# Dilated attention and a binary depthwise convolution on one core: group statistics of the packed blocks sent through DRAM, zero edges written by ScalarE, and a new table of places

## The chip, the cores and the metric

The kernel runs on one core of a Trainium2 chip. The metric is the device time of one launch in microseconds (us), taken as the median of several runs. For the kernel before the change it is 5095.06 us (three runs, 5094.93 to 5096.68). One more execution was taken with the hardware profiler; every row quoted below comes from it.

## The reference, cut to what matters

The input x has 16 images of 56 x 56 pixels and 384 channels, float32. Two layers follow each other, each with a residual:

```python
x = x + attention(_gn(x), w_qkv, w_proj, b_proj)   # layer 0
x = x + depthwise3x3(_gn(x), sign(clip(w)))        # layer 1

def _gn(v, G=32, eps=1e-5):        # no affine part; one mean and variance per image and group of 12 channels
    g = v.reshape(B, H, W, G, C // G)
    return ((g - mean(g, (1, 2, 4))) / sqrt(var(g, (1, 2, 4)) + eps)).reshape(v.shape)
```

The attention has three channel groups of 128 with dilations 1, 2 and 3. In each, four heads of 32 channels look at nine neighbours: score = sum over a head's channels of q times the shifted k, softmax over the nine, then the weighted sum of the shifted v, then a 384 x 384 projection. The convolution multiplies each channel with nine taps that are -1, 0 or 1. Outside the picture k, v and the normalised input of the convolution are zero.

## The kernel before, in words

**Chunks.** An image is cut into 7 chunks of 8 rows (448 pixels); channels lie on the partitions, in three blocks of 128. So there are 112 chunks, and each goes through three stages, written as generators:

- *A* (`plan_a`): load x (L471), transpose it on TensorE (`pt_x`, L476), copy it out (ScalarE, L489), take its statistics (VectorE, L491), store it channel-major in DRAM as `xd` (L494).
- *B* (`plan_b`): load (L520), normalise (ScalarE, L524); project k and v (`pkv`, L528, copied out by ScalarE, L541) and exchange halo rows with the chunk before by small DMAs (L549, L550); project q (`pq`); nine score products on VectorE (`t`, L593), each 128 x 1344; sum them over channels on TensorE (`ps`, L574, in bursts of 8, 8 and 11 matmuls); softmax (L613 to L648, with a transposing DMA L646); spread the weights over channels (`pb_a`, L660), multiply with v on VectorE (`w`, L671), add on GpSimd (L681 to L685); project (`po`, L699), add residual and bias (L703), take the statistics of the result (L707), store it as `x1d` (L710).
- *C* (`plan_c`), ten chunks behind B: channel blocks 0 and 1 are convolved partly on TensorE. They are loaded from `x1d` as "packed" blocks `z` of 96 partitions (L770): 32 channels in three vertically shifted copies, four sets of 32 channels beside each other. ScalarE applies scale and offset to z (L786), TensorE multiplies with diagonal matrices (`pc`, L818), VectorE adds the middle column of taps (L829 to L835). Block 2 goes over ScalarE (L860, L882) and GpSimd (L892 to L900). The result is transposed back (`pt_o`, L909), copied (L915) and stored (L918).

**Statistics.** `group_norm` turns 12-channel statistics into scale and offset per channel. It runs once per image (for layer 1 of image b and layer 0 of image b+2 together) and crosses the engines: L352 VectorE, `pm` TensorE (L358), L360 VectorE, `pb` TensorE (L365), L368 VectorE, L370 and L371 GpSimd, `pv` TensorE (L376), L380 to L384 VectorE, thirteen tiny GpSimd operations for the inverse root (L387 to L391, tile `pair`), `pp` TensorE (L396), and `mr` (L399, VectorE), which has scale and offset for each of 128 channels. The packed z needs the same numbers on 96 partitions, three times: that is `mrz`. Before the change 24 tiny matmuls compute it a second time (`pz`, L408) and VectorE copies it out of PSUM (L414).

**Zero edges.** In the first and last chunk of an image one row of z lies outside the picture. GpSimd writes zeros there after the load (L775) and again after the normalisation (L789), since the offset makes them nonzero.

**Order.** Engines execute their queues in order. The order is written out by hand: `WHEN` gives each step of each stage a place; a chunk takes nine places (STEP = 9), so a step of chunk m stands at 9m plus its place (C: 9(m + 10) plus its place). `put` registers the steps, and from place 0 to place 9 x 112 + 14 each engine is held to that order (`pin`). Only the order counts; the places are no waits. A list of several numbers belongs to one generator, which is advanced one `yield` at each. The places of `statistics` are counted from the last chunk of the image.

**Buffers.** PSUM tiles with the tag "mt" (`pkv`, `po`, `pt_x`, `pt_o`, `pc`, `pt_s` and all the statistics') share three banks; `pq`, `pb_a` and `ps` have one each. SP issues nearly all DMAs, in order, over eight semaphores in turn.

Of the kernel before, what the change touches and what calls it, by code (L numbers as in the profile page):

```python
# [8 lines left out]
F32 = mybir.dt.float32  # L9
# [8 lines left out]
P = 128  # L18
HEADS = 4
HD = 32  # L20
NG = 3
NTAP = 9
NQ = 4
# [8 lines left out]
TERMS = 3  # L32

WHEN = dict(
    load_in=[[1.86]],
    turn_in=[[6.026, 7.853, 8.103, 9.616], [8.887, 8.898, 11.431, 13.527], [9.427, 9.669, 9.841, 12.978]],
    load_x=[[-16.698]],
    normalise=[[-14.8], [-11.887], [-14.8]],
    k=[[-7.795, -7.784, -7.773], [-6.349, -6.338, -2.8], [-3.845, -3.158, -1.177]],
    v=[[7.341, 7.352, 8.827], [5.08, 6.207, 9.429], [7.847, 8.378, 9.967]],  # L40
    query=[[4.619], [7.271], [8.939]],
    score=[[4.825], [5.138], [5.149], [7.626], [7.637], [7.877], [10.723], [10.734], [10.745]],
    burst=[[5.75], [8.056], [11.108]],
    softmax=[[11.283, 12.017, 12.028, 12.151, 13.101, 13.445, 14.191, 14.202, 14.629, 15.664]],
    weigh=[[17.248, 17.838, 20.379], [18.267, 18.278, 20.39], [20.023, 20.034, 20.421], [20.194, 20.223,
        23.104], [20.709, 20.932, 24.835], [21.886, 22.889, 25.743], [23.429, 23.44, 25.754], [23.902, 25.371,
        27.079], [25.884, 25.895, 27.807]],
    load_residual=[[28.002]],
    out_project=[[28.362, 28.749, 29.829, 108.842], [28.647, 29.405, 34.465, 55.401], [30.355, 30.533, 31.612,
        34.476]],  # L50
    load_g=[[9.822]],
    normalise_g=[[10.839]],
    taps=[[11.121, 12.433], [11.132, 12.731], [11.143, 14.144]],
    sums=[[18.53], [18.541], [18.813]],
    load_x1=[[5.837]],
    load_z=[[-1.661, 3.083], [1.74, 3.075]],
    normalise_z=[[5.379, 5.39], [7.123, 7.821]],
    column=[[6.427], [7.222]],
    convolve=[[5.632, 6.438], [8.054, 8.065]],
    turn_out=[[19.405, 19.416, 19.866], [20.439, 20.499, 20.51], [21.786, 21.835, 27.008], [22.192, 22.518,  # L60
        22.582]],
    statistics=[[33.116, 34.74, 35.945, 35.956, 37.004, 37.015, 37.026, 37.993, 38.004, 39.539, 40.578, 40.589,
        40.926, 40.937, 41.368]],
)
C_SHIFT = 0
FIXED_ENGINES = ("PE", "DVE", "Activation", "Pool", "SP")
# [3 lines left out]
def dilated_attention_then_binary_conv(  # L70
# [28 lines left out]
    nc = tc.nc  # L99
    B, H, W, C = x.shape  # L100
    PX = ROWS * W
    NCH = H // ROWS
# [4 lines left out]
    K3 = 3 * HD  # L107
    JG = NG - 1
# [10 lines left out]
    ps_mt = ctx.enter_context(tc.tile_pool(name="ps_mt", bufs=3, space=PSUM))  # L119
# [5 lines left out]
    ident = const.tile([P, P], F32, name="ident")  # L125
# [13 lines left out]
    for p in range(NPAD):  # L139

        v = place(p) if p < NG * NTAP else p
# [202 lines left out]
    def group_norm(sets):  # L344

        L = len(sets)
        ch = st_p.tile([P, L, NG, 2], F32, tag=f"ch{L}", name="ch")
        for only_first in (False, True):
            for n, (stats, _, for_convolution) in enumerate(sets):
                if for_convolution == only_first:  # L350
                    for j in range(NG):
                        nc.vector.bn_aggr(ch[:, n, j, :], stats()[:, j].rearrange("p c s -> p (c s)"))  # L352
            yield

        pair = st_p.tile([GN_G, L, 3], F32, tag=f"pair{L}", name="pair")
        pm = ps_mt.tile([P, 512], F32, tag="mt", name="pm")
        for j in range(NG):
            nc.tensor.matmul(pm[:GN_G, 0:L], gsel[:, j], ch[:, :, j, 0], start=(j == 0), stop=(j == NG - 1))  # L358
        yield
        nc.vector.tensor_scalar_mul(pair[:, :, 2], pm[:GN_G, 0:L], -1.0 / GN_CH)  # L360
        yield

        pb = ps_mt.tile([P, 512], F32, tag="mt", name="pb")
        for j in range(NG):
            nc.tensor.matmul(pb[:, j * L : (j + 1) * L], gselT[:, j], pair[:, :, 2], start=True, stop=True)  # L365
        yield
        dev = st_p.tile([P, L, NG], F32, tag=f"dev{L}", name="dev")
        nc.vector.tensor_tensor(dev, pb[:, : NG * L].rearrange("p (j l) -> p l j", l=L), ch[:, :, :, 0], ALU.add)  # L368
        yield
        nc.gpsimd.tensor_tensor(dev, dev, dev, ALU.mult)  # L370
        nc.gpsimd.tensor_tensor(dev, dev, ch[:, :, :, 1], ALU.add)  # L371
        yield

        pv = ps_mt.tile([P, 512], F32, tag="mt", name="pv")
        for j in range(NG):
            nc.tensor.matmul(pv[:GN_G, 0:L], gsel[:, j], dev[:, :, j], start=(j == 0), stop=(j == NG - 1))  # L376
        yield
        var = st_p.tile([GN_G, 3, L], F32, tag=f"var{L}", name="var")
        v, r, t = var[:, 0], var[:, 1], var[:, 2]
        nc.vector.tensor_scalar(v, pv[:GN_G, 0:L], 1.0 / GN_CH, 1e-5, op0=ALU.mult, op1=ALU.add)  # L380

        ri = r.bitcast(I32)
        nc.vector.tensor_single_scalar(ri, v.bitcast(I32), 1, op=ALU.arith_shift_right)
        nc.vector.tensor_scalar(ri, ri, -1, RSQRT_BITS, op0=ALU.mult, op1=ALU.add)  # L384
        yield
        for step in range(3):
            nc.gpsimd.tensor_tensor(t, r, r, ALU.mult)  # L387
            nc.gpsimd.tensor_tensor(t, t, v, ALU.mult)
            nc.gpsimd.tensor_scalar(t, t, -0.5, 1.5, op0=ALU.mult, op1=ALU.add)
            nc.gpsimd.tensor_tensor(pair[:, :, 1] if step == 2 else r, r, t, ALU.mult)  # L390
        nc.gpsimd.tensor_tensor(pair[:, :, 0], pair[:, :, 2], pair[:, :, 1], ALU.mult)  # L391
        yield

        pp = ps_mt.tile([P, 512], F32, tag="mt", name="pp")
        for j in range(NG):
            nc.tensor.matmul(pp[:, 2 * L * j : 2 * L * (j + 1)], gselT[:, j], pair[:, :, 0:2], start=True, stop=True)  # L396
        yield
        mr = st_p.tile([P, NG, L, 2], F32, tag=f"mr{L}", name="mr", bufs=5 - L)
        nc.vector.tensor_copy(mr.rearrange("p j l s -> p (j l s)"), pp[:, : 2 * L * NG])  # L399
        yield  # L400
        mrz = None
        if sets[0][2]:

            pz = ps_mt.tile([P, 512], F32, tag="mt", name="pz")
            for s in range(JG * NQ):
                of_set = gselT[:, s // NQ, s % NQ * HD : s % NQ * HD + HD]
                for ky in range(3):
                    nc.tensor.matmul(  # L408
                        pz[ky * HD : (ky + 1) * HD, 2 * s : 2 * s + 2], of_set, pair[:, 0, 0:2], start=True, stop=True
                    )  # L410
        yield
        if sets[0][2]:
            mrz = st_p.tile([K3, JG, NQ, 2], F32, tag="mrz", name="mrz")
            nc.vector.tensor_copy(mrz.rearrange("p j q s -> p (j q s)"), pz[:K3, : 2 * JG * NQ])  # L414
        yield
        for n, (_, done, for_convolution) in enumerate(sets):
            done(mr[:, :, n], mrz) if for_convolution else done(mr[:, :, n])
# [92 lines left out]
    def plan_b(m, t0):  # L510
# [180 lines left out]
        def out_project(j):  # L691

            if c == 0 and j == 0:
                stats1[b] = st_p.tile([P, NG, NCH, 6], F32, tag="stats1", name="stats1")
                x1d[b] = dr_p.tile([C, H * W], F32, tag="x1d", name="x1d")
            xr = had["xr"]
            po = ps_mt.tile([P, 512], F32, tag="mt", name="po")
            for g in range(NG):
                nc.tensor.matmul(  # L699
                    po[:, :PX], wprojT[:, g, j * P : (j + 1) * P], had[f"y{g}"], start=(g == 0), stop=(g == NG - 1)  # L700
                )
            yield
            nc.vector.scalar_tensor_tensor(  # L703
                xr[:, j, :], po[:, :PX], bias[:, j : j + 1], xr[:, j, :], op0=ALU.add, op1=ALU.add
            )
            yield
            nc.vector.bn_stats(stats1[b][:, j, c, :], xr[:, j, :])  # L707
            yield
            if j == NG - 1:
                nc.sync.dma_start(chunk_of(x1d[b], c), xr)  # L710
# [24 lines left out]
    def plan_c(m, t0):  # L735
# [2 lines left out]
        p0 = c * PX  # L738
        had = {}

        def edges(j):
            found = []
            for z, _, _ in had[f"z{j}"]:
                if c == 0:
                    found.append(z[0:HD, :, 0:W])
                if c == NCH - 1:
                    found.append(z[2 * HD : 3 * HD, :, PX - W : PX])
            return found

        def set_of(j, q):  # L750
            return next(z[:, q - q0] for z, q0, q1 in had[f"z{j}"] if q0 <= q < q1)
# [1 line left out]
        def load(j):  # L753
# [17 lines left out]
                        z[ky * HD : (ky + 1) * HD, :, lo:hi], by_set[:, q0:q1, n0 + lo : n0 + hi]  # L771
                    )
            yield
            for edge in edges(j):
                nc.gpsimd.memset(edge, 0.0)  # L775

        def normalise(j):
            mrz = mr1[b][1]
# [6 lines left out]
                    continue  # L785
                nc.scalar.activation(z, z, AF.Identity, bias=mrz[:, j, q, 0:1], scale=mrz[:, j, q, 1:2])  # L786
            yield
            for edge in edges(j):
                nc.gpsimd.memset(edge, 0.0)  # L789

        lo, hi = (0 if c else 1), ROWS + (2 if c < NCH - 1 else 1)

# [248 lines left out]
```

## Time and profile before

| what | value |
|---|---|
| median of three runs | 5095.06 us |
| profiled execution | 5091.71 us, of it the span of the core 5089.7 us |
| busy share: PE, DVE, ACT, POOL | 96%, 87%, 49%, 84% |
| a chunk without statistics, in the middle | 42.20 us |
| the two chunks with statistics, in the middle | 43.50 and 46.70 us |
| seven chunks of an image, in the middle | 301.2 us or 302.9 us, about in turn |
| first softmax copy (L613), last one | at 110.7 us, at 4877.9 us |

The chunk times are distances between the copies of L613, of which there is one per chunk. PE, DVE, ACT, POOL and SP are TensorE, VectorE, ScalarE, GpSimd and SyncE; PEld is TensorE's weight load. A group row of the page has line, engine, operation, out<-in with shapes and count, then busy time in us and the mean of one in ns, then the idle time of the engine just before such instructions and what ended it. A float32 matmul leaves two records. In the stretches view each row is one stretch: its length, then busy time and count of instructions by engine, the granted clock of TensorE (1.00 is full), and the DMA share.

### The profile page before, as it was taken

The page shows a single profiled execution, that of the slowest core. Times are in us where ns is not written, and L with a number is a line of the kernel's source. Part 1 is how long each engine was busy: PE and PEld are TensorE (multiplying, and loading weights), DVE is VectorE, ACT ScalarE, POOL GpSimd, SP SyncE. Part 2 cuts the span into 40 slices and gives each one's busy share as a digit, 9 for nine tenths or more (in the row PEclk, how much of TensorE's full clock was granted, in tenths as well). Part 3 has the DMA queues.
Part 4 walks back from the last instruction along what each step waited for, and adds up shares of the span by engine and source line. Part 5 has one row for each costly group of instructions (what it writes and reads, how often), then busy time and mean ns, then how long its engine had stood idle before and what let it go on. Part 6 is the DMA issues. An engine that isn't in the chain of part 4 may idle for free.

```text
span 5089.7 us, 72426 instructions
## 1 busy us (share of the span) xinstructions
PE 4883.7 (96%) x25093; PEld 2242.3 (44%) x25093; DVE 4434.3 (87%) x4575; ACT 2476.1 (49%) x4365; POOL 4253.3 (84%) x2998
## 2 busy tenths in 40 slices
PE   6899999999999999999999999999999999999975
PEld 4344444444444444444444444444444444444422
DVE  3788998989989998998989899898998999888866
ACT  3122555545555455555555555454555545455445
POOL 2566888888888988988888898888888888899981
PEclk8999999999999999999999999999999999999976
DMA  5334666666666666666666566666666666555555
GB/s 161 110 111 117 171 174 173 175 174 177 175 173 170 166 176 173 177 174 172 175 167 179 160 182 173 171 176 172 176 175 173 172 167 175 152 151 148 137 131 165
DMA packets 813955, 836.43 MB, mean 164 GB/s; under 512 B 362643, under 2 KB 782870, under 8 KB 813590
## 3 DMA queue, kind: packets, MB, share of 16 engines
q1 hardware_dynamic: 805606, 819.81, 60.1%
q10 hardware_dynamic: 7984, 12.00, 0.7%
q8 instruction: 199, 3.26, 0.3%
q14 instruction: 166, 1.36, 0.1%
HBM read 477.43 MB, written 231.21 MB: 139 GB/s over the span
## 4 chain that ended last, share of the span: by engine, by line
PE 78%; DVE 6%; POOL 5%; issue 2%; ACT 2%; DMA 2%; SPq 0%; ACTq 0%; DVEq 0%; POOLq 0%
PE pkv L528 24%; PE po L699 13%; PE pq L528 13%; PE ps L574 10%; PE pc L818 6%; PE pb_a L660 5%; PE pt_o L909 3%; PE pt_x L476 3%; DVE w L671 3%; POOL w L681 2%; DVE t L593 2%; PE pt_s L617 1%; ACT z L786 1%; POOL m L892 1%; DMA z<-x1d 1%
## 5 line engine op out<-in xcount | busy, mean ns | idle before, releaser
L681 POOL TENSOR_TENSOR w<-w 128x1344 f32<-128x1344 f32 x672 | 2052.2, 3054 | 448.4 <-DVE w L671 438.4
L671 DVE TENSOR_TENSOR w<-pb_a,v 128x1344 f32<-128x1344 f32 x1008 | 1562.7, 1550 | 347.0 <-PE pb_a L660 302.5
L593 DVE TENSOR_TENSOR t<-pq,k 128x1344 f32<-128x1344 f32 x1008 | 1512.8, 1545 | 56.5 <-PE pq L528 46.3
L528 PE MATMUL pkv<-xn,wqkvT 128*128 128x448 f32 x3924 | 1553.8, 541 | 0.0
L528 PEld LDWEIGHTS pkv<-xn,wqkvT 128*128 128x128 f32 x3924 | 727.8, 190 | 648.0 <-issue 617.6
L699 PE MATMUL po<-y,wprojT 128*128 128x448 f32 x2016 | 824.6, 546 | 18.6 <-POOL y L685 18.0
L528 PE MATMUL pq<-xn,wqkvT 128*128 128x448 f32 x1962 | 811.4, 550 | 0.0
L574 PE MATMUL ps<-t,sel 128*32 128x448 f32 x6048 | 664.7, 549 | 36.6 <-DVE t L593 36.4
L892 POOL TENSOR_TENSOR m<-m 128x1344 f32<-128x1344 f32 x210 | 639.0, 3043 | 10.8 <-ACT m L882 1.5
L786 ACT ACTIVATE z<-z,mrz 96x448 f32<-96x448 f32 x840 | 570.2, 751 | 101.8 <-DVE mrz L414 97.1
L882 ACT ACTIVATE m<-zg,ktap 128x448 f32<-128x448 f32 x945 | 540.4, 655 | 9.8 <-ACT zg L860 0.4
L541 ACT COPY v<-pkv 128x448 f32<-128x448 f32 x336 | 179.0, 533 | 742.2 <-DVE w L671 380.7
L699 PEld LDWEIGHTS po<-y,wprojT 128*128 128x128 f32 x2016 | 369.2, 192 | 320.0 <-issue 283.2
L528 PEld LDWEIGHTS pq<-xn,wqkvT 128*128 128x128 f32 x1962 | 350.3, 192 | 253.8 <-issue 253.5
L541 ACT COPY k<-pkv 128x448 f32<-128x448 f32 x336 | 180.1, 536 | 547.2 <-PE pkv L528 547.2
L685 POOL TENSOR_TENSOR y<-y,w 128x448 f32<-128x448 f32 x336 | 381.8, 1136 | 26.3
L684 POOL TENSOR_TENSOR y<-w 128x448 f32<-128x448 f32 x336 | 381.3, 1135 | 26.2
L660 PE MATMUL pb_a<-aT,spread 24*128 24x448 bf16 x3024 | 369.5, 360 | 20.6 <-DVE w L671 18.6
L660 PEld LDWEIGHTS <-spread 24*128 24x128 bf16 x3024 | 100.3, 91 | 636.8 <-issue 627.5
L489 ACT COPY xa<-pt_x 128x448 f32<-128x448 f32 x315 | 167.8, 534 | 433.7 <-PE pt_x L476 406.0
L818 PE MATMUL pc<-z,kdiag 96*32 96x440 f32 x3360 | 358.0, 544 | 16.5 <-POOL z L789 15.5
L574 PEld LDWEIGHTS ps<-t,sel 128*32 128x32 f32 x6048 | 190.4, 110 | 390.6 <-issue 293.4
(141 smaller groups left out, 4649.7 us busy)
## 6 DMA issues: line engine op xcount, KB each, us to landing
z<-x1d SPq DMA_DIRECT2D x570, 224.0 KB, 5.2
xr<-xd SPq DMA_DIRECT2D x112, 672.0 KB, 4.5
x1d<-xr SPq DMA_DIRECT2D x112, 672.0 KB, 5.4
xn<-xd SPq DMA_DIRECT2D x109, 672.0 KB, 4.9
xin<-in_x_dram SPq DMA_DIRECT2D x105, 672.0 KB, 8.2
xd<-xa SPq DMA_DIRECT2D x315, 224.0 KB, 2.6
out_dram<-osb SPq DMA_DIRECT2D x420, 168.0 KB, 2.4
x<-x1d SPq DMA_DIRECT2D x80, 560.0 KB, 4.2
```

Of the source, the lines that this page charges most:

```text
L528: nc.tensor.matmul(dst[:, :PX], wqkvT[:, cc, o0 : o0 + P], had["xn"][:, cc, :], start=(cc == 0), stop=(cc == NG - 1))
L574: return nc.tensor.matmul(had["ps"][32 * j : 32 * j + 32, :PX], sel[:, s0 : s0 + 32], tk, start=(issued[j] == 1), stop=(issued[j] == len(r ...
L593: nc.vector.tensor_tensor(t.rearrange("p k (r w) -> p k r w", w=W), q3, k3, ALU.mult)
L660: return nc.tensor.matmul(pb[:, kx, :PX].rearrange("p (s n) -> p s n", s=NSUB), spread[rows_of, v % 2, :], had["a"][rows_of, :, v // 8, :] ...
L671: nc.vector.tensor_tensor(w.rearrange("p k (r w) -> p k r w", w=W), pb[:, :, :PX].rearrange("p k (r w) -> p k r w", w=W), three(kv[1][g][m ...
L681: nc.gpsimd.tensor_tensor(w0, w0, w, ALU.add)
L685: nc.gpsimd.tensor_tensor(y, y, w0[:, 2], ALU.add)
L699: nc.tensor.matmul(po[:, :PX], wprojT[:, g, j * P : (j + 1) * P], had[f"y{g}"], start=(g == 0), stop=(g == NG - 1))
L786: nc.scalar.activation(z, z, AF.Identity, bias=mrz[:, j, q, 0:1], scale=mrz[:, j, q, 1:2])
L818: return nc.tensor.matmul(pcr[q * HD : (q + 1) * HD, :, x0:x1], kdiag[:, kx // 2, j * NQ + q, :], rows(set_of(j, q))[:, :, x0 + kx - 1 : x ...
L882: nc.scalar.activation(rows(t[:, kx]), zp[:, ky : ky + ROWS, kx : kx + W], AF.Copy, scale=ktap[:, JG, o : o + 1])
L892: nc.gpsimd.tensor_tensor(had["m"], had["m"], t, ALU.add)
```

## The change

- `mrz` is no longer computed by `pz`. SP writes the first two channel blocks of `mr` to a DRAM tile `mrd` (128 x 2 x 2 numbers), and in the next step reads it back into `mrz` with three DMAs, one for each vertical shift.
- `zero` replaces `edges`: ScalarE copies a block of zeros out of the identity matrix into the edge, at the same two steps. Nothing of the packed blocks is left on GpSimd.
- `out_project` looks up the residual tile one step later, so that the projection may stand ahead of the residual's load.
- All places are new. The numbers in the diff are of the steps that the text speaks of.

```diff
-    k=[[-7.795, -7.784, -7.773], [-6.349, -6.338, -2.8], [-3.845, -3.158, -1.177]],
+    k=[[-1.772, -1.287, -0.448], [0.602, 0.693, 0.86], [1.389, 1.4, 3.364]],
-    query=[[4.619], [7.271], [8.939]],
-    score=[[4.825], [5.138], [5.149], [7.626], [7.637], [7.877], [10.723], [10.734], [10.745]],
+    query=[[8.972], [10.387], [12.844]],
+    score=[[9.067], [9.078], [9.773], [10.398], [11.394], [12.106], [13.128], [13.334], [13.447]],
...
-    load_x1=[[5.837]],
-    load_z=[[-1.661, 3.083], [1.74, 3.075]],
-    normalise_z=[[5.379, 5.39], [7.123, 7.821]],
-    column=[[6.427], [7.222]],
-    convolve=[[5.632, 6.438], [8.054, 8.065]],
+    load_x1=[[12.088]],
+    load_z=[[4.532, 8.639], [18.154, 18.373]],
+    normalise_z=[[11.361, 11.372], [19.211, 19.222]],
+    column=[[12.191], [16.571]],
+    convolve=[[12.055, 12.746], [20.473, 20.484]],
...
-    statistics=[[33.116, 34.74, 35.945, 35.956, 37.004, 37.015, 37.026, 37.993, 38.004, 39.539, 40.578, 40.589,
-        40.926, 40.937, 41.368]],
+    statistics=[[38.5, 42.48, 42.607, 43.359, 44.23, 44.622, 44.633, 44.887, 45.025, 45.117, 45.558, 45.569,
+        45.58, 46.991, 47.002]],
...
         mrz = None
         if sets[0][2]:
-
-            pz = ps_mt.tile([P, 512], F32, tag="mt", name="pz")
-            for s in range(JG * NQ):
-                of_set = gselT[:, s // NQ, s % NQ * HD : s % NQ * HD + HD]
-                for ky in range(3):
-                    nc.tensor.matmul(
-                        pz[ky * HD : (ky + 1) * HD, 2 * s : 2 * s + 2], of_set, pair[:, 0, 0:2], start=True, stop=True
-                    )
+            mrd = dr_p.tile([P, JG, 2], F32, tag="mrd", name="mrd")
+            nc.sync.dma_start(mrd, mr[:, :JG, 0, :])
         yield
         if sets[0][2]:
             mrz = st_p.tile([K3, JG, NQ, 2], F32, tag="mrz", name="mrz")
-            nc.vector.tensor_copy(mrz.rearrange("p j q s -> p (j q s)"), pz[:K3, : 2 * JG * NQ])
+            for ky in range(3):
+                nc.sync.dma_start(
+                    mrz[ky * HD : (ky + 1) * HD], mrd.rearrange("(q c) j s -> c j q s", c=HD)
+                )
...
-            xr = had["xr"]
             po = ps_mt.tile([P, 512], F32, tag="mt", name="po")
...
             yield
+            xr = had["xr"]
             nc.vector.scalar_tensor_tensor(
...
-        def edges(j):
-            found = []
+        def zero(j):
             for z, _, _ in had[f"z{j}"]:
                 if c == 0:
-                    found.append(z[0:HD, :, 0:W])
-                if c == NCH - 1:
-                    found.append(z[2 * HD : 3 * HD, :, PX - W : PX])
-            return found
+                    edge, lo = z[0:HD, :, 0:W], 0
+                elif c == NCH - 1:
+                    edge, lo = z[2 * HD : 3 * HD, :, PX - W : PX], 2 * HD
+                else:
+                    continue
+                at_ = 0 if lo else 2 * HD
+                none = ident[lo : lo + HD, at_ : at_ + W].unsqueeze(1)
+                nc.scalar.copy(edge, none.to_broadcast([HD, edge.shape[1], W]))
...
-            for edge in edges(j):
-                nc.gpsimd.memset(edge, 0.0)
+            zero(j)
```

TensorE's order of one chunk in the middle, before and after (x3 and so on are matmuls; the chunk begins with the softmax's transposes):

```
before: pt_s4 po3 pt_o3 pb_a3 pt_o3 pq3 pkv6 pb_a3 pc8 ps8 pb_a3 pt_x4 pq3 pkv6 pb_a3 pc8 ps8 pb_a3 pt_x4 pq3 pb_a3
        pt_x4 pkv3 po3 pt_o3 po3 pb_a3 ps11 pb_a3 pt_o3 pkv3 pb_a3
after:  pt_s4 pkv3 pq3 pb_a3 pt_o3 pt_o3 po3 pkv3 pt_o3 pt_x4 pb_a3 pt_x4 pt_o3 pq3 pkv3 pb_a3 ps8 pc8 pb_a3 pkv6 pb_a3
        pc8 ps8 pb_a3 pq3 po6 pb_a3 ps11 pb_a3 pkv3 pb_a3 pt_x4
```

The statistics' groups on TensorE stand before: pm ahead of a pb_a, pb one group later, pv after the last po, and in the next chunk pp after the second pt_o, then pq3, pz24. After: pm ahead of the last pkv; in the next chunk pt_s4, pb, pkv3, pv, pq3 pb_a3 pt_o3 pt_o3 po3, pp, pkv3.

## The prediction on record

> **What bounds the kernel now.** I read the busy shares and slices first, then stretches of single chunks, then TensorE's timeline where a chunk is longer, then the waits.
>
> ```profile
> PE 4883.7 (96%) x25093; PEld 2242.3 (44%) x25093; DVE 4434.3 (87%) x4575; ACT 2476.1 (49%) x4365; POOL 4253.3 (84%) x2998
> ...
> PE   6899999999999999999999999999999999999975
> ...
> PEclk8999999999999999999999999999999999999976
> ```
>
> PE is busy at 90% or more from the third slice to the 38th; only there can time be won in bulk. Busy is not yet full, so next come three stretches in the middle: a plain chunk and the two with statistics.
>
> ```profile
> 1618.70:1660.90 42.20, 42.20 (x215) 19.25 (x214) 38.84 (x38) 22.30 (x40) 37.20 (x22) 1.00 0.68 179
> 1660.90:1704.40 43.50, 42.69 (x229) 19.88 (x227) 39.97 (x49) 22.42 (x41) 37.81 (x37) 1.00 0.64 172
> 1704.40:1751.10 46.70, 45.11 (x271) 21.23 (x272) 39.38 (x41) 23.01 (x43) 42.10 (x32) 1.00 0.60 161
> ```
>
> In a plain chunk PE has no gap: 42.20 of 42.20 us, and its groups follow each other at fixed distances (three accumulated float32 matmuls every 2.26 us). So a plain chunk is worth what TensorE issues. The two chunks with statistics take 1.3 and 4.5 us more, 5.8 per image. TensorE's timeline shows where the second part is lost:
>
> ```profile
> 1705.27 0.83 PE L396 MATMUL pp<-pair,gselT 32*128 32x4 f32 x6 [1.57 <-POOL pair L391]
> 1706.03 2.52 PE L528 MATMUL pq<-xn,wqkvT 128*128 128x448 f32 x6
> 1708.48 0.68 PE L408 MATMUL pz<-pair,gselT 32*32 32x2 f32 x48
> ...
> 1714.88 1.68 PE L818 MATMUL pc<-z,kdiag 96*32 96x440 f32 x16 [0.72 <-POOL z L789]
> ```
>
> pp stands idle for the end of GpSimd's inverse root, and pc for GpSimd's zero edge. The waits of the whole run say that this is so for every image:
>
> ```profile
> ACT z L786 <- DVE mrz L414: 97.1, 15, 7.6
> ...
> POOL z L789 <- ACT z L786: 41.2, 15, 8.4
> ...
> PE pp L396 <- POOL pair L391: 30.9, 17, 4.0
> ```
>
> (total us, times, longest). In nearly every second image something follows that no wait shows:
>
> ```profile
> 2006.48:2007.90 1.42, 1.42 (x8) 1.22 (x9) 1.00 (x3) 1.03 (x3) 1.42 (x1) 1.00 0.08 22
> 2007.90:2011.30 3.40, 3.40 (x5) 1.02 (x4) 0.15 (x1) 0.00 (x0) 3.32 (x2) 0.50 0.83 229
> ```
>
> The granted clock falls to 0.50 for 3.4 us right behind the late pp. That image takes 302.9 us instead of 301.2.
>
> **What the Trainium skill says.** "TensorE: Matmul & The Clock Gate", section "What's actually happening": the clock is halved after a window of about 3.4 us with little activity and restored after a busy one; the windows run freely. The trace agrees (0.50 for 3.4 us), and free windows explain why only some images are hit. "DMA: Bandwidth & Descriptors", section "Anatomy of one DMA": about 2.0 us are fixed, most of it the receipt of the last write. The shortest median from issue to landing here is 1.8 us (k halo, 29 KB). The same page, section "Two DMAs through the same engine are not ordered": a dependent DMA must be issued behind a wait for the first one's semaphore, so SP itself will wait for `mrd`; no row of before shows such a pair.
>
> **The change part by part.** One set of statistics per image, 16 in all, 15 of them beside dense PE work.
>
> *pz leaves TensorE.* From pq's start to pz 2.45 us and from pz to pkv 0.605; without pz, pq to pkv is 2.27. Gain 0.79 x 15 = 11.8 us. L414's 0.16 us on VectorE is covered by PE.
>
> *pp's wait.* 1.84 us from the transpose ahead of it, 0.11 where nothing is missing: 1.73 x 15 = 26.0 us, if the new places cover it. Now pv to pp are pq, pb_a, two pt_o and a po: 0.3 + 2.37 + 0.30 + 0.70 + 2.35 = 6.0 us. Between them must fit: pv's result (0.4), VectorE's three small operations (0.55), GpSimd's root, which in the trace runs from 1701.85 to 1705.21 (3.35 us), and what GpSimd has ahead of the root: one of L897 and L900, 2.3 us behind L371. L371 ends some 0.6 us ahead of pv's turn, so the root begins at +1.6 us and pp may start at +5.0: covered, 1 us to spare. pv itself has only a pkv (2.26 us) behind pb in which VectorE (L368) and GpSimd (0.5 us) must answer: they do by about 1.7. What is late next is the w that GpSimd adds between root and softmax rest; aT is issued at about 15 us from the chunk's start instead of 11, lands after 4.0 us (its median), and pb_a needs it at 23.
>
> *The half clock.* Seven such windows begin at a pp (499, 1404, 2008, 2612, 3216, 3820 and 4718 us). At 1.67 us each: 11.7 us. They go with the wait.
>
> *pc's wait.* 1.08 us against 0.29 after a pb_a: 0.79 x 15 = 11.8 us. What takes its place is `mrz` through DRAM. From the chunk's start (pt_s): pp at 9.7, mr at 10.8, so SP issues `mrd` at 11. In SP's order out, two halo DMAs, aT, xd, x1d and two halo DMAs stand between it and `mrz`; aT waits for GpSimd until 15, and at 1.5 us for aT and about 0.5 for each other, the three `mrz` go at 18.9 to 19.9. SP's wait for `mrd` is covered by aT. Landing: 256 runs of 8 bytes each. The nearest rows are 384 single numbers in 5.1 us (small, 1.5 KB) and the fixed 2.0 us; I take 4.3 between them. So `mrz` is there at 24.2. ScalarE then does four z (0.65 apart), one xn and the edge, and pc can start at 28.1. The edge has no row: a copy of 448 takes 0.534 us and one of 384 0.469, so 224 take about 0.31, and I bound it by 0.28 (GpSimd's memset) and 0.53. PE reaches this pc at 25.9 plus 2.1 of statistics = 28.0. With 2.0 for the landing pc waits for nothing, with 5.1 for 0.9. I charge 0.5 x 15 = 7.5 us. Queued behind z on ScalarE are two copies of v, u and the nine tap products; their readers on PE come 5 us later.
>
> *Edges off GpSimd.* 136 memsets, 0.28 us each: 34 us of GpSimd time, but PE sets the pace, so nothing beyond pc's wait. ScalarE is at 49%; it gains the same count at 0.31. In the tail GpSimd's four waits for z_last (22.7 us) go, too.
>
> *New places in plain chunks.* The same groups stand on PE. Summed with the distances of before: twelve projections at 2.26, nine pb_a at 0.30, ps 1.5 + 1.5 + 2.27, two pc at 1.5, pt_x 3 x 0.44, pt_o 1.4, pt_s 0.49, and 0.1 for each of eight changes from float32 to pb_a: 42.2 us, as before. Gain nothing, if nothing is late. I followed the tightest cover: the second pq stands at 12.6 us from pt_s and needs the third t of the first group. VectorE starts mx at 0.64, then sub, bn, w, sum, reciprocal (5.28), t, mul, t, residual, w, and the third t from 10.8 to 12.4. Slack 0.2 us. I charge 0.05 x 100 chunks = 5 us.
>
> *Start and end.* Chunks ahead of the first C chunk are about 40.2 us now although PE has 37.3 us of work; their waits are for t, and the new order shortens them by my ledger by about 0.5: gain 4 us. In the tail two DMA hops stand between mr and z_last (about +7), and against it the column scalars are computed ahead of GpSimd's tap sums and the waits for zero edges are gone (-7). I take 0 with 12 either way.
>
> Sum: -11.8 - 26.0 - 11.7 - 11.8 + 7.5 + 5 - 4 = -52.8; half of the residual doubts of fifteen sets (0.3 us more each for a late link of the chain) gives back 5: -48. Against the profiled execution, 5091.7 - 48 = 5043.7; the median lies 3.35 us above that execution, so 5047.
>
> **The rivals.**
>
> *The hop is slow.* If `mrz` needs 8 us to land (the 1152 numbers of 4.5 KB took 10.6), pc waits 3.8 us, and the gap halves the clock in every second image (1.67): 15 x (3.8 - 0.5) + 7 x 1.67 = 61 us back: 5108 at that end, 5083 at 6 us of landing. For it: `mrd` and `mrz` are of 8-byte runs, and DMA engines are 64% busy. Against: few bytes, and 5.1 us was measured at the kernel's start beside large loads. I take 5083 for this case.
>
> *The plain chunk stalls (slower).* The place is the second pq behind the third t. If VectorE's run from mx to that t ends over 0.2 us later than I count, PE waits in each of about 105 chunks; from 0.66 us (a stall of 0.46) the 48 us are gone, and at 0.9 the time is 5047 + 0.7 x 105 = 5120. For it: VectorE is busy 38.84 of 42.20 us and has five kinds of work in this run, with ScalarE's exponential and copies between. Against: each of its distances is measured, and the order of before, as tightly laid, has no gap at all.
>
> *Better than that.* No residual wait, and start and end gain what the waits there show: 5030.
>
> *The change does not do what it says* can't be for pz and the edges: they are gone from the orders.
>
> **How the numbers follow.** Forecast 5047: 0.60, own range 5032 to 5064. Better, 5030: 0.10. Slow hop, 5083: 0.15, about half of it within the band. Stalling chunk, 5120: 0.15. A measurement of this kernel can tell about 0.2% (10 us) from no change. So faster 0.60 + 0.10 + 0.08 = 0.78, same 0.07, slower 0.15. The range leaves out most of the slower case and the end of the better one: 5024 to 5098.
>
> **What would show it.** Plain chunks of 42.2 us; an image of about 298.5 instead of 301.2 or 302.9; no L408 group; pp no longer waiting for pair; no 0.50 window behind pp; pc waiting under 1 us for z; `mrz` landing in 3 to 5 us. I am wrong if pq or ps wait for t in every chunk, if z waits for DMA mrz far beyond 24 us from pt_s, or if the tail behind the last softmax copy (212 us now) grows by over 15.

## The result and the profile after

The changed kernel takes 5064.3 us, the median of six runs (5061.2 to 5066.8). Beside runs of the kernel before on the same chip (median 5096.4, six runs) the ratio is 0.994, with a 95% interval of 0.992 to 0.995. It is faster by about 32 us; 48 had been forecast. The profiled execution took 5065.0 us (span 5063.3), against 5091.7 for that of before: these 26.7 us are what the parts below are held against. One of the five runs with ScalarE's edges alone, at 9224 us and a granted clock of 0.817, was in a slow state; the ratio of that kernel is of the other four.

The busy lines of the page, as shown of before (engines with us, share and count; then tenths in 40 slices):

```profile
PE 4883.1 (96%) x24325; PEld 2249.2 (44%) x24325; DVE 4455.8 (88%) x4559; ACT 2524.2 (50%) x4501; POOL 4224.4 (83%) x2862
...
PE   7899999999999999999999999999999999999965
...
PEclk9999999999999999999999999999999999999976
```

TensorE is as long busy as before, in a shorter span. The 768 small matmuls of pz, 11.4 us of busy time before, are gone, but the others together are busy that much longer. The three stretches, from pt_s to pt_s (a chunk with the first of the statistics, the chunk with all the rest, a plain chunk; span and PE's busy time first):

```profile
1929.38:1971.98 42.60, 42.60 (x221) 19.70 (x220) 40.10 (x46) 23.83 (x43) 37.49 (x21) 1.00 0.64 176
1971.98:2018.30 46.32, 44.98 (x234) 20.96 (x233) 39.65 (x43) 24.24 (x45) 40.02 (x39) 1.00 0.69 162
2018.30:2060.60 42.30, 42.30 (x215) 19.45 (x214) 39.16 (x40) 22.82 (x41) 37.92 (x24) 1.00 0.67 179
```

Statistics now cost 0.3 us over a plain chunk in one chunk and 2.4 to 4.0 in the next, instead of 1.7 and 4.2 to 5.9. The plain chunk has no gap but is 0.1 us longer than before. TensorE's timeline in the middle chunk (start, us, then in brackets the idle time and who ended it):

```profile
1981.82 0.83 PE L397 MATMUL pp<-pair,gselT 32*128 32x4 f32 x6
1982.57 2.52 PE L526 MATMUL pkv<-xn,wqkvT 128*128 128x448 f32 x6
...
1994.61 1.69 PE L817 MATMUL pc<-z,kdiag 96*32 96x440 f32 x16 [1.19 <-ACT z L749]
...
2001.75 1.68 PE L817 MATMUL pc<-z,kdiag 96*32 96x440 f32 x16 [0.15 <-ACT z L749]
```

pp follows its po at the ordinary distance of 0.47 us, in all fifteen images of the middle, and no window of clock 0.50 begins between 200 and 4790 us. The second pc, whose blocks need `mrz`, is 0.15 us late. The first, which still belongs to the previous image and doesn't need this `mrz`, is 1.19 us late; over fifteen images this first wait is anything from nothing to 1.4.

Where the time went, from the starts of the score transpose pt_s in both traces (us):

| stretch | before | after | difference |
|---|---|---|---|
| start to the first pt_s | 112.9 | 104.4 | -8.5 |
| nine chunks without convolution | 378.9 | 371.8 | -7.2 |
| the other 102 chunks | 4387.3 | 4356.3 | -31.0 |
| last pt_s to the end | 210.5 | 230.8 | +20.3 |
| span | 5089.7 | 5063.3 | -26.4 |

Two thirds of what the middle gains are given back at the end.

### The profile page after: what moved, and what is told of

It is laid out like the page before. It is cut to its first block, busy times and chain, and to the rows that moved or that the text cites. A ratio compares the mean times of both kernels' runs of the same rounds, so it can differ in the third digit from the quotient of the medians.

```text
span 5063.3 us, 70210 instructions
## 1 busy us (share of the span) xinstructions
PE 4883.1 (96%) x24325; PEld 2249.2 (44%) x24325; DVE 4455.8 (88%) x4559; ACT 2524.2 (50%) x4501; POOL 4224.4 (83%) x2862
## 4 chain that ended last, share of the span: by engine, by line
PE 86%; DVE 4%; DMA 4%; POOL 2%; ACT 2%; SPq 2%; issue 1%; ACTq 0%; DVEq 0%; POOLq 0%
PE pkv L526 27%; PE pq L526 15%; PE po L696 14%; PE ps L572 11%; PE pc L817 6%; PE pb_a L658 5%; PE pt_x L474 3%; PE pt_o L908 3%; DVE t L591 2%; DMA xd<-xa 1%; DVE w L669 1%; PE pt_s L615 1%; ACT z L786 1%; POOL w L679 1%; DMA mrz<-mrd 0%
## 5 line engine op out<-in xcount | busy, mean ns | idle before, releaser
L591 DVE TENSOR_TENSOR t<-pq,k 128x1344 f32<-128x1344 f32 x1008 | 1542.2, 1549 | 100.6 <-PE pq L526 98.8
L526 PE MATMUL pkv<-xn,wqkvT 128*128 128x448 f32 x3924 | 1593.0, 547 | 0.0
L696 PE MATMUL po<-y,wprojT 128*128 128x448 f32 x2016 | 808.3, 546 | 8.8 <-POOL y L683 8.8
L891 POOL TENSOR_TENSOR m<-m 128x1344 f32<-128x1344 f32 x210 | 639.6, 3046 | 27.3 <-ACT m L881 19.1
L611 ACT COPY sT<-ps 128x448 f32<-128x448 f32 x112 | 59.8, 534 | 894.8 <-PE ps L572 894.8
L526 PEld LDWEIGHTS pq<-xn,wqkvT 128*128 128x128 f32 x1962 | 354.4, 190 | 312.7 <-issue 300.4
L658 PE MATMUL pb_a<-aT,spread 24*128 24x448 bf16 x3024 | 368.9, 359 | 23.9 <-DVE w L669 22.6
L914 ACT COPY osb<-pt_o 112x384 f32<-112x384 f32 x420 | 199.1, 474 | 291.9 <-PE pt_o L908 284.3
L636 POOL TENSOR_TENSOR rest<-ew,e 112x512 f32<-112x512 f32 x112 | 129.9, 1159 | 240.1 <-ACT e L633 240.1
```

The lines of the kernel that those rows point to most:

```text
L526: nc.tensor.matmul(dst[:, :PX], wqkvT[:, cc, o0 : o0 + P], had["xn"][:, cc, :], start=(cc == 0), stop=(cc == NG - 1))
L591: nc.vector.tensor_tensor(t.rearrange("p k (r w) -> p k r w", w=W), q3, k3, ALU.mult)
L658: return nc.tensor.matmul(pb[:, kx, :PX].rearrange("p (s n) -> p s n", s=NSUB), spread[rows_of, v % 2, :], had["a"][rows_of, :, v // 8, :] ...
L696: nc.tensor.matmul(po[:, :PX], wprojT[:, g, j * P : (j + 1) * P], had[f"y{g}"], start=(g == 0), stop=(g == NG - 1))
L891: nc.gpsimd.tensor_tensor(had["m"], had["m"], t, ALU.add)
```

## The experiments

Times are medians; ratios, with their 95% intervals, are to the kernel before on the same chip (5092 to 5094 us there). The theory at the outset: the new places take the waits away, the hop through DRAM is paid at the end, ScalarE's edges hardly matter.

### The three parts, each undone or done alone

**New places alone**: the table of places of after in the kernel before, with the later lookup of the residual tile; pz on TensorE and edges by GpSimd.

```
-WHEN = dict(load_in=[[1.86]], ...
+WHEN = dict(load_in=[[16.753]], ...
```

> The kernel before with the new places alone: pz stays on TensorE, the zero edges on GpSimd. Theory A (the places give the gain of the middle; the DRAM hop makes the end longer): the start gains about 16 us as in the changed kernel, the waits of pp and pc and the half clock go, pz still costs 0.79 us an image, the plain chunk is 42.30 us, and the stretch behind the last softmax copy stays near 212 us: in all 5053 to 5060. Theory B (the longer end comes with the new places, whose last image is planned 5.6 steps later): that stretch is about 230 us here too, and the time about 5075.

Measured: 5131.6 us, ratio 1.007 (1.006 to 1.009). Slower than before, against both theories. The start gained its 17 us, pp waits no more, but the 102 chunks took 4431 us instead of 4387. GpSimd's waits show why (line waited for: us in all, times, longest):

```profile
POOL z L790 <- ACT z L787: 228.9, 60, 10.2
```

In front of its memset of the zero edge GpSimd stands and waits for ScalarE's scaled block, 60 times, 3.8 us in the mean. In the kernel before the same memset had 41.2 us, 15 times.

**The changed kernel with pz again**:

```
-            mrd = dr_p.tile([P, JG, 2], F32, tag="mrd", name="mrd")
-            nc.sync.dma_start(mrd, mr[:, :JG, 0, :])
+            pz = ps_mt.tile([P, 512], F32, tag="mt", name="pz")
+            ...
```

> The changed kernel with scale and offset of the packed blocks made on TensorE again (pz), places and ScalarE's edges kept. Theory A (the hop is worth 0.79 us an image on TensorE, costs about 0.2 us an image at the pc behind z, and makes the end 20 us longer): +12 - 3 - 20, so about 5053. Theory B (the end is longer because of places or edges): +12 - 3, so about 5073, and the stretch behind the last softmax copy stays at 233 us.

Measured: 5060.1 us, ratio 0.994 (0.992 to 0.995): from the changed kernel it can't be told apart. An image in the middle takes 299.9 us every time, against 298.8 to 300.4 with the hop; the stretch behind the last pt_s is 221.9 instead of 230.8. So in these two profiles the hop wins some 4 us in the chunks and loses 9 at the end, and all in all it is worth nothing that the runs can tell. The end stays 11 us longer than before without it: that rest isn't the hop's.

**The changed kernel with GpSimd's edges again**:

```
-            zero(j)
+            for edge in edges(j):
+                nc.gpsimd.memset(edge, 0.0)
```

> The changed kernel with the zero edges written by GpSimd again. Theory A (edges are worth little, since PE sets the pace): 5060 to 5070. Theory C (ScalarE's edge of 0.37 us, ahead of the first pc of a chunk with statistics, is what makes that pc late, and ScalarE's edge behind VectorE's scaled block is what makes the end late): the first pc waits 0.3 us less or not at all, the end is 10 to 20 us shorter: 5042 to 5052. If GpSimd's queue delays the pc instead: over 5070.

Measured: 5153.8 us, ratio 1.011 (1.010 to 1.013); over 5070 as in the last clause, in a size that no theory had, and it is pb_a more than pc that waits. One memset, followed through the timelines of GpSimd, VectorE and TensorE:

```profile
1715.61 0.28 POOL L787 MEMSET z<- 32x224 f32 x1 [5.44 <-ACT z L784]
1715.97 3.04 POOL L679 TENSOR_TENSOR w<-w 128x1344 f32<-128x1344 f32 x1
```

```profile
1719.04 1.56 DVE L669 TENSOR_TENSOR w<-pb_a,v 128x1344 f32<-128x1344 f32 x1 [4.05 <-POOL w L679]
```

```profile
1720.65 0.56 PE L658 MATMUL pb_a<-aT,spread 24*128 24x448 bf16 x3 [3.03 <-DVE w L669]
1721.14 7.37 PE L526 MATMUL pkv<-xn,wqkvT 128*128 128x448 f32 x12
```

The memset itself is 0.28 us. But GpSimd works in order: for 5.44 us it stands before a block that ScalarE hasn't scaled yet, and the addition of w behind it is late by that. VectorE waits 4.05 us for a w buffer, TensorE 3.03 us for the bank that VectorE should have read. Then the gap is paid a second time: from 1719.6 on the granted clock is 0.50 for 6.8 us, and the pkv behind it takes 7.37 us, in the changed kernel 4.78. This chunk takes 51.8 us. In the whole run pb_a waits 59.6 us for w, in the changed kernel 22.6, and twelve windows of half clock, 68 us together, begin between 200 and 4790 us; at half of what TensorE is busy in them (an estimate) they cost 29 us.

**The hop alone, at the old places**: the two pieces of pz in before become the two DMA pieces.

> The kernel before with the DRAM hop alone, at the old places. Theory A (the hop needs about 8 us from pp to the landed mrz; the old places leave it about 6.4): pz gone -12, pc 1.8 us later in each image +27, more half clock +10, the end +20: about 5140. Theory D (the hop is free wherever it stands, the transfer is short): -12 to -24 from pz and the edges of pc: 5075 to 5085.

Measured: 5126.3 us, ratio 1.006 (1.005 to 1.008), nearer to the first theory in the chunks, but the end is not 20 us longer: 211.9 us instead of 210.5. pc is 1.2 to 4.9 us later than normal in fourteen of fifteen images, and the clock is halved somewhere in each.

**ScalarE's edges alone, at the old places**:

> The kernel before with the zero edges on ScalarE alone, at the old places. Theory A: pc no longer waits for GpSimd's memset (its gap of 1.08 us was 0.79 over the normal one), but ScalarE's edge takes 0.37 us itself behind the fourth z, so at most 0.4 us an image are won: -6, and the half clock behind pp stays: 5088 to 5096. Theory C (the edge on ScalarE costs at every first pc and in the end): 5100 to 5115.

Measured: 5072.6 us, ratio 0.996 (0.995 to 0.997): a gain of 21 us, more than either theory had. Where the clock isn't halved, pc's distance is still 1.1 us (1.08 in before), now behind ScalarE's edge: what pc waited for was the fourth z and an edge behind it, whichever engine writes it. pp's distance falls from 1.84 to 1.42, since in before two of the memsets, 0.50 us, stood directly ahead of the root in GpSimd's order. The half clock costs as much as before (five windows in the 102 chunks instead of seven, two of them twice as long). These chunks take 4377.2 us, 10 less than before, and the end is 5.7 us shorter.

**Hop and ScalarE's edges, at the old places**:

> The kernel before with the DRAM hop and ScalarE's edges at the old places (the sixth of the combinations of the three parts; places with both is the changed kernel). If the parts add up, hop +33 and edges -21: 5105. If the hop's loss at the old places is GpSimd waiting in its memset for blocks that come late, most of it goes with the memset: 5072 - 12 + 1.5 x 15 + 9, so about 5092.

Measured: 5120.2 us, ratio 1.006 (1.004 to 1.007): neither guess, and the memset is not the reason. ScalarE's wait for the transfer, in all:

```profile
ACT z L785 <- DMA mrz<-mrd: 111.7, 15, 9.3
```

pc's distance becomes 1.8 to 4.4 us. `mrz` lands after only 2.3 us in the median, but it is the second of two transfers in a row: `mrd` takes 3.5 us to land, and SyncE issues the three `mrz` (0.65 us apart) only then. At the old places SyncE stands and waits for that; in the changed kernel other work covers all but 0.9 us of it:

```profile
SPq L409 <- DMA mrd<-mr: 47.0, 16, 3.8
```

So in most images `mrz` is there 8 to 9.4 us behind pp; the old places begin z at once and PE needs pc soon after. Between 200 and 4790 us begin 22 windows of half clock, of 3.4 or 6.8 us; ten were counted in before and none in the changed kernel. By the same estimate those in the 102 chunks cost 39 us here and 12 with ScalarE's edges alone, so some 27 of the hop's 48 us are half clock. This is the clock gate of the Trainium skill ("TensorE: Matmul & The Clock Gate", section "What's actually happening": the clock is halved after an idle window of about 3.4 us, and the windows run freely). The traces agree that the windows run freely: in each run all of them begin on one grid of 3.41 us. They don't agree that the window must be idle, and here the measurement decides: in the kernel before TensorE was idle for 39 to 57% of the grid window ahead of each of the ten. With its gap of 1.6 us, pp was hit in the six images where the gap fell into one window (46% idle), and in none of the eight where the grid cut it in two (36% at most in either window). In the other runs the border is less sharp: 32% was enough in one place, and 53% was not in another.

Together, medians in us:

| | old places | new places |
|---|---|---|
| pz, edges GpSimd | 5093.5 | 5131.6 |
| hop, edges GpSimd | 5126.3 | 5153.8 |
| pz, edges ScalarE | 5072.6 | 5060.1 |
| hop, edges ScalarE | 5120.2 | 5064.3 |

Only one part gains alone. With pz, the places cost 38 us with GpSimd's edges and gain 12 with ScalarE's; with ScalarE's edges, the hop costs 48 us at the old places and at the new ones nothing that can be told from noise.

### Is it ScalarE, or the memset's place?

The changed kernel with GpSimd's edges, each memset behind a scaled block later in GpSimd's order, by 0.67 and 1.24 places:

```
-    normalise_z=[[11.361, 11.372], [19.211, 19.222]],
+    normalise_z=[[11.361, 12.04], [19.211, 20.46]],
```

> The changed kernel with GpSimd's memsets, as in the run that came to 5154 us, but each memset behind the scaled block stands 0.25 to 0.65 of a step later in GpSimd's order. If the loss there is GpSimd standing in order behind ScalarE's scaled block (240 us of waiting, 57 times), the wait falls below 100 us and the time to 5075 to 5100. Rival (the loss is not that wait, or the later memset is itself what pc then waits for): 5130 or more, with pc waiting for the memset in many chunks.

Measured: 5066.4 us, ratio 0.995 (0.994 to 0.996), where the same memsets at the earlier place gave 5153.8. GpSimd's wait:

```profile
POOL z L787 <- ACT z L784: 83.7, 31, 9.7
```

instead of

```profile
POOL z L787 <- ACT z L784: 240.1, 57, 9.7
```

So the 87 us are the wait in GpSimd's order, with the half clock that it brings (no such window begins between 200 and 4790 us here), and nothing else of that part. ScalarE's edges are one way to be rid of it, a later place is as good, although the first pc of the chunk now stands 0.77 us late behind the memset.

### The late first pc

Its cause in the changed kernel, from ScalarE's timeline in the same chunk:

```profile
1991.00 0.53 ACT L487 COPY xa<-pt_x 128x448 f32<-128x448 f32 x1 [3.86 <-DMA xd<-xa]
1991.43 2.72 ACT L786 ACTIVATE z<-z,mrz 96x448 f32<-96x448 f32 x4
1994.18 0.37 ACT L749 COPY z<-ident 32x224 f32<-32x224 f32 x1
```

The third copy to xa must wait until one of two buffers has been stored. That store was issued at 1981.68 behind three loads of z, and ScalarE is released 9.3 us later (in the two plain chunks that follow, the copy starts 4.4 and 4.8 us behind the issue); four z and the edge queue behind it, and pc behind them. The store ahead of the loads instead:

```
-    turn_in=[[17.144, 17.155, 17.527, 18.442], ...
+    turn_in=[[17.144, 17.155, 17.527, 18.15], ...
```

> The changed kernel with the store of the first transposed third (xd) issued ahead of the three loads of z instead of behind them. Theory A (in a chunk with statistics the first pc is late because ScalarE's third copy to xa waits for that store, 8.8 us from its issue): the wait of xa for xd, 45.6 us in all, falls below 10, the first pc's gap is 0.36 in every image, -7: about 5057. Rival (the pc is late by ScalarE's own work or by z's load): xa waits no more, but the first pc's gap stays up to 1.7 us: 5064 +- 3; with z later by 0.5 us even 5066.

Measured: 5051.6 us, ratio 0.992 (0.991 to 0.994), about 13 us under the changed kernel. The first pc's distance is 0.36 in every image, the second's 0.29 in twelve of fifteen; an image in the middle takes 298.8 us (299.0 once). xa waits for xd no more; ScalarE now waits 42.7 us in all for z's loads, which TensorE doesn't feel. The second pc gains with it: `mrz`, behind that delay in SP's order too, is now issued some 10.6 us (11.4 at most) behind pp instead of up to 12.6. Why the store takes so long in this chunk alone is not settled; with pz instead of the hop (5060.1 us) xa's wait was 16.8 us instead of 45.6 and the first pc was late in two images only, so the hop takes part in it.

### The longer end

pz for the last image alone:

```
         if sets[0][2]:
+            if len(mr1) == B - 1:
+                pz = ps_mt.tile([P, 512], F32, tag="mt", name="pz")
+                ...
+            else:
...
```

> The changed kernel, but the last image alone gets scale and offset by pz on TensorE. Theory A (the two hops make the end 20 us longer, since the scaled blocks come later and VectorE's own block is queued behind the taps): the stretch behind the last softmax copy falls from 233 to about 213 us, the rest does not move: 5044. Theory B (the end is longer because of places or edges): within 3 us of 5064.

Measured: 5049.1 us, ratio 0.992 (0.990 to 0.993). The end falls from 230.8 to 221.6 us, about half of what was expected. VectorE in the end of the changed kernel, and in this one:

```profile
4934.47 0.16 DVE L400 COPY mr<-pp 128x6 f32<-128x6 f32 x1 [4.97 <-PE pp L397]
...
4965.47 1.77 DVE L782 TENSOR_SCALAR z_last<-z_last,mrz 96x448 f32<-96x448 f32 x4
```

```profile
4932.56 0.17 DVE L400 COPY mr<-pp 128x6 f32<-128x6 f32 x1 [4.98 <-PE pp L397]
4933.54 0.17 DVE L419 COPY mrz<-pz 96x16 f32<-96x16 f32 x1 [0.81 <-PE pz L409]
4933.75 0.93 DVE L794 TENSOR_SCALAR z_last<-z_last,mrz 96x448 f32<-96x448 f32 x2
```

VectorE scales its blocks of the last image 31 us behind mr with the hop and 1.2 us behind it with pz. The end lies beyond the fixed order: there the scheduler places the work, and with `mrz` by DMA it has put three rounds of nine tap products ahead of those blocks. ScalarE's edges of the last image, and pc (16.2 us of waiting), queue behind them. It takes the new places for that: at the old ones the hop lengthens the end by 1.4 us alone and by 4.0 beside ScalarE's edges (204.8 to 208.8).

For what is left, the last image's statistics were planned directly behind its last bn_stats and its convolution 3.2 steps earlier, together with both cures:

```
...
+            for i in range(15):
+                at(t0 + 37.5 + .01 * i, lambda: next(steps, None))
...
```

> As the run with both edits, and the last image's statistics planned directly behind its last bn_stats, its convolution 3.2 steps earlier. If what is left of the longer end (about 11 us over before) comes from the late plan of the new places: 8 to 12 us less than with both edits, about 5026. Rival (the end is set by loads of z and the taps on VectorE, whatever the plan): within 3 us of the run with both edits, or longer, since statistics now stand ahead of the last stores.

Measured: 5054.4 us, ratio 0.993 (0.992 to 0.994), 13 us worse than both cures alone. The end grew from 219.7 to 230.1; pp now waited 11.6 us for the root, whose small operations stood between tap sums in GpSimd's order. So planning earlier is no cure as it stands; why the end with both cures is still 9 us longer than before stays open.

### The longer plain chunk

The changed kernel, with one transpose group put between a pb_a and the projection behind it (and its load ahead of it):

```
-    turn_in=[[17.144, ...
+    turn_in=[[16.2, ...
```

> The changed kernel with one transpose group (pt_x of the first third) moved ahead of the projection that stands directly behind a pb_a, and its load ahead of it. Theory A (a float32 projection directly behind a pb_a starts 0.10 us late, behind a transpose 0.05 us are lost instead): the first distance of that pkv falls from 0.48 to 0.38, pt_s's rises by 0.05, so a plain chunk falls from 42.30 to 42.25 us and about 80 chunks give -4: 5060. Rival (the pace of a plain chunk is set elsewhere, or the earlier transpose holds a PSUM bank too long): 42.30 stays, or it grows by a wait of pt_x or pkv, 5064 to 5080.

Measured: 5082.0 us, ratio 0.998 (0.997 to 0.999). The first distance of that pkv, from its first matmul to its second, fell as foreseen, from 0.48 to 0.39, but the plain chunk only from 42.30 to 42.28, since pt_s now stands behind the pb_a. And once in most images a pkv now waits up to 1.5 us until VectorE has read a po; that the earlier transpose takes one of the three PSUM banks which they share is the likely reason.

```profile
PE pkv L526 <- DVE xr L701: 20.8, 14, 1.5
```

The distance is confirmed; the cure cost more than the loss.

### A faster version

The changed kernel with pz for the last image and the earlier store:

> The changed kernel with two edits at once: pz on TensorE for the last image alone, and xd stored ahead of the loads of z. If the two gains are of separate places (the end, 9 us less there; the first pc of chunks with statistics, 8 to 14 us less), they add up: 5064 - 15 - 13, so about 5036. If they share a cause: 5042 to 5050.

Measured: 5041.4 us, ratio 0.990 (0.989 to 0.992); it beats both kernels. The images take 298.8 to 299.0 us, the end 219.7. The two gains nearly add up (23 of 28).

## Why the prediction was right, and where not

Forecast 5047 (5024 to 5098), measured 5064: the sign and the mechanism at pp are as forecast, the gain is two thirds of it. By its steps, for the 102 chunks (forecast -44 with the doubts, measured -31), the start and the end:

- *pz leaves TensorE*, -12: right. Where nothing else was late (the run with the earlier store) an image takes 298.8 us against 299.9 with pz: 1.1 us, forecast 0.79.
- *pp's wait*, -26: right, gone in every image. The working (pair ready 1 us before pp) held: 0.8 us in the middle.
- *pc's wait for GpSimd's edge*, -12: gone, but by the places: with ScalarE's edges at the old places it stayed. These three parts together were forecast at 3.3 us an image. The images without half clock took 301.2 us before and 298.8 where nothing was late; with the 0.1 us that seven chunks lost (below) the parts gained about 3.1.
- *The half clock*, -12: right. It went with the gaps, stayed where pp still stood at 1.42, and multiplied where pc stood longer.
- *pc's wait for mrz*, +7.5: measured 4.3, and only 1.5 in the run with the earlier store. That the charge came out close is luck in part: two terms of its working were off and cancelled. `mrz` is issued later than reckoned, 19.1 to 22.4 us from pt_s instead of 18.9, since aT and the late xd hold SP longer; and it lands in a median of 2.2 us (2.1 to 2.7), half of the 4.3 taken between 2.0 and 5.1:

```profile
DMA to landing us min/median/max: 2.1/2.2/2.7
```

  The short end was right: the fixed cost of about 2.0 us of "DMA: Bandwidth & Descriptors" in the Trainium skill, section "Anatomy of one DMA" (given there for DMAs that GpSimd issues; these are SyncE's), is about all there is for 256 runs of 8 bytes. At 6 us of landing the prediction's own sum gives 5078, not 5083.
- *The first pc*: a term that was missing, +6. The prediction followed the pc that needs `mrz`, and not the one ahead of it, whose blocks wait for ScalarE, and ScalarE for a store.
- *Plain chunks*, +5 for a wait at the third t: some +16, and for another reason. With input loads pq hardly waits. The time is in TensorE's own order, as its timeline shows: the same six matmuls take 0.10 us more directly behind a pb_a.

```profile
2018.30 0.60 PE L615 MATMUL pt_s<-perm,sT 128*112 128x128 f32 x4
2018.73 2.42 PE L526 MATMUL pkv<-xn,wqkvT 128*128 128x448 f32 x6
...
2057.12 0.36 PE L658 MATMUL pb_a<-aT,spread 24*128 24x448 bf16 x3
2057.41 2.52 PE L526 MATMUL pkv<-xn,wqkvT 128*128 128x448 f32 x6
```

  In before a transpose stood between pb_a and every projection of a plain chunk; now three projections stand directly behind one. Three times 0.10 is lost; three times 0.05 is won back, since three transposes fewer stand behind a pb_a, and another 0.05 in smaller differences: 0.1 in each of some 90 chunks. The ledger had one price for a change of group, whatever stood on its two sides. The stall at the third t did come, 0.6 us in nine of the last chunks: there the input transposes ahead of pq are missing, and with them the slack. Most of these take 41.85 us against 41.14 before, some 7 us more in all. The steps so far add up to about -46 - 12 + 4 + 6 + 16 = -32; -31 was measured.
- *The start*, -4: measured -16. The direction was right; what brings the rest wasn't divided further. It comes with the places (-17 with them alone). The 12 us beyond the forecast are luck, and they pay for more than half of what the end loses.
- *The end*, 0 with 12 either way: measured +20, and this was named as a sign of being wrong. The prediction added two hops in time, +7, but beyond the fixed order the hop at the new places changes the order itself (9 us, by the run with pz there). The other 11 us are not explained; most of them come with the places (218.8 us with them alone).
- *Edges at nothing* beyond pc's wait: wrong, though the total doesn't show it. The prediction took the memset's 0.28 us, and PE as the cover. It passed over two memsets ahead of the root, and so of pp (0.42 us an image), and never priced the wait in GpSimd's queue. At the old places that wait was 41 us in all, and ScalarE's edges alone gain 21; at the new ones it is 240, and GpSimd's memsets put back into the changed kernel cost 89.

The rivals. *The slow hop* is real at the old places, and so is the half clock that it foresaw behind it, but not by a landing of 6 or 8 us: by two short landings in a row for which these places leave no time. *The stalling plain chunk* came in nine late chunks and six early ones instead of a hundred. The forecast attributed the gain to parts that add up; the table of the eight combinations shows that they don't.

## What to carry to other kernels

On an engine that works in order, an operation costs what stands behind it while it waits, not its own length: follow the queue to the engine that sets the pace before you write zero. When a change has several parts, price each with and without the others: here new places lose 38 us or gain 12, as a 0.28-us memset stands in one queue or not. Count what a gap brings with it: of the hop's 48 us at the old places some 27 were, by the estimate above, the half clock behind the gaps. And follow the piece ahead of the one you changed: the wait that took the place of the removed one belonged to the previous image's pc.

## What was not expected of the hardware

- A float32 projection of 128 columns takes 0.48 us to its second matmul directly behind the bf16 pb_a, 0.38 to 0.39 behind a transpose; ps and pc with their 32 columns show no such delay behind pb_a (1.50 us for pc in both kernels).
- A DMA of 256 runs of 8 bytes landed in a median of 2.2 us, about like the two kinds of 29-KB halo DMAs of the same kernel (2.4 and 3.2), while the loads and stores of xd on the same queue (224 to 672 KB) took from 1.9 to 9.2 us:

```profile
DMA to landing us min/median/max: 1.9/4.7/9.2
```
